# A Mamba layer's input projection as one product a half, with the causal convolution's taps on ScalarE and VectorE

## The chip, the cores and the metric

The kernel runs on one core of one Trainium2 chip. The metric is the time of one execution on the device in microseconds (us). A profile is one execution taken by the hardware profiler; PE is TensorE, DVE is VectorE, ACT is ScalarE, POOL is GpSimd, SP is SyncE, whose queue issues the DMAs.

## What is computed

Two "metaformer" layers over an image of 4 x 128 channels x 64 x 64. Layer 0 is a deformable neighbourhood attention, then a sigmoid recurrence over the 4,096 positions. Layer 1 is a stack of eight Mamba layers, then a mixture of experts. Only the Mamba layer is changed:

```
xz = x @ Wi                                  # (B, L, 128) @ (128, 512)
xi, z = split(xz, 2)                         # 256 inner channels each
xp = pad(xi, 3 zeros ahead along L)
xc = silu(sum(xp[:, k:k+L, :] * cw[:, k] for k in range(4)) + cb)
dt, Bs, Cs = from xc @ Wx                    # dt through softplus
h_t = exp(dt A) h_(t-1) + dt xc Bs           # 16 states per inner channel, a scan along L
y = (sum over states of h Cs + D xc) * silu(z)
out = y @ Wo, then RMS norm
```

Everything is float32.

## The kernel before

Four stages follow each other: the attention (`conv_layer`), the recurrence, `mamba`, the experts. The first two and the last are ordered by a scheduler, `mamba` is not: there each engine executes its instructions in the order of the program.

Channels lie on the 128 partitions, positions along the free dimension, in chunks of 512 (`TL`). The 256 inner channels are two halves (`h` = 0, 1). The unit of work is a body: one chunk, one layer, one image; there are 8 chunks x 8 layers x 4 images = 256 bodies. A body's work is spread over three turns of the main loop: `front(n, j)` prepares body n while body o = n - 1 is scanned, and `last(q, j)` finishes body q = o - 1. A turn has 16 slots (`j`); slot j handles two of the 16 states for one half:

- `decay` (L650, ScalarE) writes dA = exp(dt A) for slot j + 2, into four buffers;
- `inputs` (L664, TensorE) writes dt xc Bs into PSUM (dBx, two buffers of two banks) for slot j + 1, from `dtxT` and the block diagonal `diag`;
- `scan` (L679, VectorE) runs two scans into `hs`, from dA in SBUF and dBx in PSUM;
- `times_c` (L691 and L694, GpSimd) keeps the last state and multiplies `hs` by C, which lies in `Cb`;
- `add_up` (L715, TensorE) adds the products of slot j - 2 into `yT` in PSUM by transposing them. `skips` (L702) starts that sum in slot 2 with D xc, by a diagonal matrix.

Between these stand the steps of `front` and `last`. In `front`: `halo` (L532 and L533, GpSimd) puts the last three inputs of the chunk before in front of u, the layer's normalized input, and keeps this chunk's last three in `tail`; `proj` (L540, TensorE) makes projection and convolution of a half in one PSUM bank, as four products, one for each tap, each of a weight matrix already scaled by the tap with u shifted by one position. Two of them stand in each of slots 0, 1 (first half) and 3, 4 (second half). `silu` (L548 to L556) comes in slot 5, `xproj` (L563) in 6, `step_proj` (L587) in 8, `softplus` (L594) in 9, `turn_b` (L623) and `step_x` (L603, GpSimd) in 10, `diag` (L635, VectorE) in 11 and 12, `turn` (L613, L618) in 12 and 13. In `last`: `leave` (L729, ScalarE) copies `yT` in slot 1, `turn_back` transposes it (L735) and multiplies it by the gate on VectorE (L736) in slots 2 and 6, `out_proj` (L742 to L748) is in slot 7, `rms` (L752) in 10, `rms_u` (L757) in 11. All these PSUM results share two banks (`bank()`).

The tap-scaled weights are made once at the start: `mamba_weights` loads, for each layer, the projection and the taps spread over all partitions, multiplies them on GpSimd (L415), makes the diagonal matrices of D on VectorE (L419), and stores both to DRAM in `made_d` (L426), from which `load` fetches `made` and `given` for every layer, once in four bodies. These DMAs stand in SyncE's queue ahead of the first stage's own weights (L117 to L128). The first stage's depthwise convolution (L192) is a chain of 48 VectorE instructions a block, each of which reads two SBUF tensors.

Of the kernel before, what the change touches and what calls it, by code (L numbers as in the profile page):

```python
# [8 lines left out]
F32 = mybir.dt.float32  # L9
AF = mybir.ActivationFunctionType  # L10
ALU = mybir.AluOpType
# [6 lines left out]
P = 128  # L18
B = 4
# [18 lines left out]
DEPTH = 8  # L38
NH = 2
DI = NH * P  # L40
NS = 16
RK = 8
DC = 4
TL = 512
# [350 lines left out]

W_CONV, W_D, W_MADE = 0, DC * DI, DC * DI + NH * P
W_Z, W_X, W_DT, W_OUT, W_GIVEN = 0, DI, DI + NH * P, 2 * DI + NH * P, 2 * DI + 2 * NH * P


def mamba_weights(tc, ops, I, made_d):

    nc = tc.nc
    with tc.tile_pool(name="mw", bufs=2) as w:
        skip = w.tile([P, DEPTH, NH], F32, name="skip", bufs=1)
        nc.sync.dma_start(out=skip, in_=I["m_skip"])
        for l in range(DEPTH):
            wi = w.tile([P, DI], F32, tag="wi", name="wi")
            nc.sync.dma_start(out=wi, in_=I["m_in"][l])  # L410
            taps = w.tile([P, DC, DI], F32, tag="taps", name="taps")
            nc.sync.dma_start(out=taps, in_=I["m_taps"][l].partition_broadcast(P))
            made = w.tile([P, W_MADE], F32, tag="made", name="made")
            for t in range(DC):
                nc.gpsimd.tensor_tensor(  # L415
                    made[:, W_CONV + t * DI : W_CONV + (t + 1) * DI], wi, taps[:, t, :], ALU.mult
                )
            for h in range(NH):
                nc.vector.tensor_scalar(  # L419
                    made[:, W_D + h * P : W_D + (h + 1) * P],  # L420
                    ops.ident,
                    skip[:, l, h : h + 1],
                    None,
                    ALU.mult,
                )
            nc.sync.dma_start(out=made_d[l], in_=made)  # L426

# [9 lines left out]
def mamba(tc, ops, I, made_d, x2_d, x3_d):  # L437
# [7 lines left out]
    nc = tc.nc  # L445
# [3 lines left out]
    with ExitStack() as ctx:  # L449
        c = ctx.enter_context(tc.tile_pool(name="mc", bufs=1))  # L450
        wp = ctx.enter_context(tc.tile_pool(name="mwp", bufs=2))
        w1 = ctx.enter_context(tc.tile_pool(name="mw1", bufs=1))
        w = ctx.enter_context(tc.tile_pool(name="mwk", bufs=2))
# [3 lines left out]
        up = ctx.enter_context(tc.tile_pool(name="mu", bufs=6))  # L457
# [5 lines left out]
        cb = c.tile([P, DEPTH, NH], F32, name="cb")  # L463
# [9 lines left out]

        i64 = c.tile([P, 64], F32, name="i64")
        nc.vector.tensor_tensor(i64, ops.ident[:, 0:64], ops.ident[:, 64:P], ALU.add)

        tail = c.tile([P, DEPTH, B, DC - 1], F32, name="tail")
        nc.vector.memset(tail, 0.0)
        state = c.tile([P, DEPTH, B, NH, NS], F32, name="state")
        nc.vector.memset(state, 0.0)  # L480

        T0 = DC - 1
        us = {}
        weights = {}

        def bank():
            return psf.tile([P, TL], F32, tag="f", name="f")
# [28 lines left out]
            rstd(o.var, ops.eps6)  # L516

        def start_d(o):
            us[o.b] = up.tile([P, T0 + TL], F32, tag="u", name="u")
            nc.vector.tensor_tensor(us[o.b][:, T0:], o.xm, o.var, ALU.mult)  # L520

        def rstd(v, eps):

# [2 lines left out]
            nc.scalar.activation(v, r, AF.Exp, scale=-0.5)  # L526


        def halo(o):
            o.made, o.given = weights[o.l]  # L530
            o.u = us[o.b]
            nc.gpsimd.tensor_copy(o.u[:, 0:T0], tail[:, o.l, o.b, :])  # L532
            nc.gpsimd.tensor_copy(tail[:, o.l, o.b, :], o.u[:, TL : TL + T0])  # L533
            o.px = {}

        def proj(o, h, t):
            if t == 0:
                o.px[h] = bank()
            at = W_CONV + t * DI + h * P
            nc.tensor.matmul(  # L540
                o.px[h], o.made[:, at : at + P], o.u[:, t : t + TL], start=t == 0, stop=t == DC - 1
            )

        def silu(o):
            o.xc = w.tile([P, NH, TL], F32, tag="xc", name="xc")
            o.gate = w.tile([P, NH, TL], F32, tag="gate", name="gate", bufs=3)
            for h in range(NH):
                nc.scalar.activation(  # L548
                    o.xc[:, h, :], o.px[h], AF.Silu, bias=cb[:, o.l, h : h + 1]
                )  # L550
            for h in range(NH):
                pz = bank()
                at = W_Z + h * P
                nc.tensor.matmul(pz, o.given[:, at : at + P], o.u[:, T0:], start=True, stop=True)
                nc.scalar.activation(o.gate[:, h, :], pz, AF.Silu)
            nc.scalar.preload_act_table_set(EXP_LN)  # L556

# [24 lines left out]
        def step_proj(o):  # L582
            o.pt = {}
            for h in range(NH):
                o.pt[h] = bank()
                at = W_DT + h * P
                nc.tensor.matmul(  # L587
                    blocks(o.pt[h]), o.given[:, at : at + P], o.dbl, start=True, stop=True
                )
# [39 lines left out]
        def diag(o, n):  # L629

            if n == 0:
                o.diag = w.tile([P, NB, NS // 2, 64, 2], F32, tag="diag", name="diag")
            for k in range(2):
                at = n * P + RK + k
                nc.vector.tensor_tensor(  # L635
                    o.diag[:, n, :, :, k],
                    o.BT[:, at : at + NS : 2].unsqueeze(2).to_broadcast([P, NS // 2, 64]),
                    i64.unsqueeze(1).to_broadcast([P, NS // 2, 64]),
                    ALU.mult,
                )  # L640
# [55 lines left out]
        def skips(o):  # L696

            o.yT = psy.tile([P, NH, NB, P], F32, tag="yT", name="yT")
            for h in range(NH):
                at = W_D + h * P  # L700
                for n in range(NB):
                    nc.tensor.matmul(  # L702
                        o.yT[:, h, n, :],
                        o.xc[:, h, n * P : (n + 1) * P],
                        o.made[:, at : at + P],
                        start=n == 0,
                        stop=True,
                        skip_group_check=True,
                    )
# [43 lines left out]
            rstd(o.pm, ops.eps5)  # L753

        def rms_u(o):
            us[o.b] = up.tile([P, T0 + TL], F32, tag="u", name="u")
            nc.vector.tensor_tensor(us[o.b][:, T0:], o.pos, o.pm, ALU.mult)  # L757

        def end(o):
            here = (slice(None), o.b, slice(o.ck * TL, (o.ck + 1) * TL))  # L760
            x3 = w1.tile([P, TL], F32, tag="x3", name="x3")
            nc.sync.dma_start(out=x3, in_=x2_d[here])
            nc.gpsimd.tensor_tensor(x3, x3, us[o.b][:, T0:], ALU.add)
            nc.sync.dma_start(out=x3_d[here], in_=x3)


# [6 lines left out]
        def front(n, j):  # L773

            if j == 0:
                halo(n)
            if j in (0, 1):
                proj(n, 0, 2 * j)
                proj(n, 0, 2 * j + 1)
            elif j in (3, 4):  # L780
                proj(n, 1, 2 * (j - 3))
                proj(n, 1, 2 * (j - 3) + 1)
            elif j == 5:
                silu(n)
            elif j == 6:
                xproj(n)
            elif j == 8:
                step_proj(n)
            elif j == 9:
                softplus(n)  # L790
            elif j == 10:
                turn_b(n)
                step_x(n)
            elif j == 12:
                turn(n, 0)
            elif j == 13:
                turn(n, 1)
            if 11 <= j <= 12:
                diag(n, 2 * (j - 11))
                diag(n, 2 * (j - 11) + 1)  # L800
            if 8 <= j:
                give_c(n, j - 8)

        def last(q, j):

            if j == 1:
                leave(q)
            elif j == 2:
                turn_back(q, 0)
            elif j == 6:  # L810
                turn_back(q, 1)
            elif j == 7:
                out_proj(q)
            elif j == 10:
                rms(q)
            elif j == 11:
                rms_u(q)
            elif j == 12 and q.l == DEPTH - 1:
                end(q)
# [16 lines left out]
        for j in range(NSLOT):  # L836
            front(bodies[0], j)
# [3 lines left out]
        for i in range(len(bodies) + 1):  # L841
            o, n, q, s = get(i), get(i + 1), get(i - 1), get(i + 2)
# [210 lines left out]
def layouts(a):  # L1053
# [3 lines left out]
    def halves(v):  # L1057
        return np.moveaxis(v.reshape(DEPTH, NH, P, *v.shape[2:]), 2, 0)

    f = {k: np.asarray(v) for k, v in a.items()}  # L1060
    o = {}
# [16 lines left out]
    o["offw"] = offw  # L1078
    o["mask"] = attention_masks()
    w_in = f["L1_conv_W_in"]  # L1080
    o["m_in"] = w_in[:, :, :DI]
    o["m_taps"] = f["L1_conv_conv_w"].transpose(0, 2, 1)
    given = np.zeros((DEPTH, P, W_GIVEN), np.float32)
    given[:, :, W_Z : W_Z + DI] = w_in[:, :, DI:]
    for h in range(NH):
        ch = slice(h * P, (h + 1) * P)
# [9 lines left out]
    gate = np.zeros((P, 2, P), np.float32)  # L1096
# [24 lines left out]
```

## Time and profile before

| what | value |
|---|---|
| time, median of 3 runs | 24,200.53 us (24,181.13 to 24,201.42) |
| the profiled execution: its own time | 24,197.25 us |
| its span, from first to last instruction | 24,195.5 us |
| mean granted TensorE clock | 0.811 |
| busy over the span: PE, DVE, POOL, ACT | 83%, 56%, 50%, 45% |
| scans (L679) in the Mamba stage | 8,192, from 7,403.8 us on |

A line of the groups reads: line, engine, operation, output <- inputs by name, shapes, count | busy us, mean ns of one | idle time of the engine just before them, and what ended it. A line of the waits reads: who waited <- for whom: us in total, times, longest. A line of the timeline reads: start, duration, engine, line, operation. Two kinds of TensorE instruction are counted for each float32 product that is no transpose, so a product is two MATMUL instructions.

### The profile page before, as it was taken

How to read it: one execution, taken by the hardware profiler on the slowest of the kernel's cores; microseconds unless marked ns; L12 is line 12 of the kernel's file. 1: busy time of each engine (PE TensorE's matmuls, PEld its weight loads, DVE VectorE, ACT ScalarE, POOL GpSimd, SP SyncE). 2: the span in 40 equal slices, each digit the busy share in tenths (PEclk: the TensorE clock that was granted, in tenths of full speed). 3: DMA queues.
4: the chain of work that ended last, by engine and by line, in shares of the span. 5: the costliest groups of instructions: out<-in, count | busy, mean ns of one | idle time of the engine just before them, and what ended most of it. 6: DMA issues, size and time to landing. Idle time of an engine off the chain costs nothing. (4 is left out here: it accounts for less than half of the span.)

```text
span 24195.5 us, 332916 instructions
## 1 busy us (share of the span) xinstructions
PE 20047.8 (83%) x133890; PEld 14387.8 (59%) x133890; DVE 13649.9 (56%) x14587; ACT 10831.4 (45%) x19815; POOL 12077.8 (50%) x10464
## 2 busy tenths in 40 slices
PE   4775867666668899989898998989898898989887
PEld 2442435555556666666666666666666666666665
DVE  6446350000005777777777777777777777777771
ACT  2332332222224555555555555555555555555551
POOL 3122120000005666666666666666666666666661
PEclk6665655555558999999999999999999999999996
DMA  0000000000001222222222212222221222222223
GB/s 28 12 8 7 13 6 11 8 7 8 7 6 65 73 72 79 72 74 76 74 73 72 79 69 77 76 74 72 74 77 70 75 76 74 74 76 73 72 75 93
DMA packets 501522, 1334.68 MB, mean 55 GB/s; under 512 B 86416, under 2 KB 170000, under 8 KB 499856
## 3 DMA queue, kind: packets, MB, share of 16 engines
q1 hardware_dynamic: 499984, 1313.37, 15.7%
q8 instruction: 1063, 17.42, 0.3%
q14 instruction: 475, 3.89, 0.0%
HBM read 1257.59 MB, written 55.57 MB: 54 GB/s over the span
## 5 line engine op out<-in xcount | busy, mean ns | idle before, releaser
L679 DVE TENSOR_TENSOR_SCAN hs<-dA,state,dBx 128x512 f32<-128x512 f32 x8192 | 9856.6, 1262 | 2837.8 <-PE dBx L664 2354.5
L694 POOL TENSOR_TENSOR hs<-hs,Cb 128x1024 f32<-128x1024 f32 x4096 | 9655.6, 2357 | 329.3 <-POOL state L691 3.7
L664 PEld LDWEIGHTS dBx<-diag,dtxT 64*128 64x128 f32 x65536 | 4206.2, 196 | 3026.9 <-issue 1765.9
L650 ACT ACTIVATE dA<-dt,A 128x512 f32<-128x512 f32 x8192 | 5317.1, 715 | 1263.8 <-DVE hs L679 1243.8
L664 PE MATMUL dBx<-diag,dtxT 64*128 64x128 f32 x65536 | 5013.0, 294 | 826.2 <-DVE hs L679 825.2
L715 PE MATMUL yT<-ident,hs 128*128 128x128 f32 x32768 | 4653.8, 289 | 4.4 <-POOL hs L694 4.4
L715 PEld LDWEIGHTS yT<-ident,hs 128*128 128x128 f32 x32768 | 3704.9, 146 | 507.5 <-issue 81.7
L388 PE MATMUL p<-y,vt 128*128 128x4 f32 x8192 | 2411.8, 365 | 1069.0 <-ACT y L391 1069.0
L691 POOL COPY state<-hs 128x2 f32<-128x2 f32 x4096 | 768.6, 188 | 4751.5 <-DVE hs L679 4696.5
L540 PE MATMUL f<-u,made 128*128 128x512 f32 x4096 | 2366.7, 708 | 787.8 <-POOL u L532 787.8
L388 PEld LDWEIGHTS p<-y,vt 128*128 128x128 f32 x8192 | 2063.1, 313 | 1460.1 <-ACT y L391 1439.9
L391 ACT ACTIVATE y<-p 128x4 f32<-128x4 f32 x4096 | 711.2, 174 | 2826.2 <-PE p L388 2826.2
L393 POOL TENSOR_TENSOR x<-x,y 128x512 f32<-128x512 f32 x32 | 48.9, 1529 | 3497.8 <-ACT y L391 3497.8
L379 DVE TENSOR_SCALAR wx<-wx,sc,sh 128x512 f32<-128x512 f32 x32 | 17.5, 546 | 2975.6 <-DMA wx<-wx_d 2975.6
L540 PEld LDWEIGHTS f<-u,made 128*128 128x128 f32 x4096 | 798.5, 216 | 1464.6 <-POOL u L532 848.3
L729 ACT COPY yTs<-yT 128x512 f32<-128x512 f32 x512 | 274.9, 589 | 2743.1 <-PE yT L715 2743.1
L736 DVE TENSOR_TENSOR y<-f,gate 128x512 f32<-128x512 f32 x512 | 354.3, 692 | 1661.3 <-PE f L735 1661.3
L635 DVE TENSOR_TENSOR diag<-f,i 128x512 f32<-128x512 f32 x2048 | 1265.7, 684 | 12.7 <-PE f L623 12.7
L192 DVE SCALAR_TENSOR_TENSOR acc<-qp,dww,acc 128x512 f32<-128x512 f32 x1536 | 1177.7, 827 | 2.6
L618 ACT COPY dtxT<-f 128x512 f32<-128x512 f32 x512 | 300.1, 586 | 1218.0 <-PE f L613 1217.9
L296 PEld LDWEIGHTS pa<-vk,at 110*128 110x128 f32 (+1 forms) x3072 | 597.9, 289 | 201.6 <-ACT exps L280 125.7
L603 POOL TENSOR_TENSOR dtx<-dt,xc 128x512 f32<-128x512 f32 x512 | 648.0, 1288 | 18.6 <-ACT dt L594 18.6
(196 smaller groups left out, 16886.0 us busy)
## 6 DMA issues: line engine op xcount, KB each, us to landing
Cb<-c_d SPq DMA_DIRECT2D x2048, 512.0 KB, 4.1
x<-x_d SPq DMA_DIRECT2D x160, 256.0 KB, 2.9
made<-made_d SPq DMA_DIRECT2D x64, 640.0 KB, 5.6
given<-in_m_given_dram SPq DMA_DIRECT2D x64, 512.0 KB, 6.3
w<-in_w_dram SPq DMA_DIRECT2D x128, 256.0 KB, 2.7
x_d<-x SPq DMA_DIRECT2D x96, 256.0 KB, 2.0
xb<-in_x_dram SPq DMA_DIRECT2D x32, 256.0 KB, 2.6
xr<-in_x_dram SPq DMA_DIRECT2D x32, 256.0 KB, 2.7
```

What stands on the lines that cost most here:

```text
L192: nc.vector.scalar_tensor_tensor(rows(acc), qp[:, r + dy : r + dy + ROWS, dx : dx + W], dww[:, t : t + 1], rows(acc), ALU.mult, ALU.add,)
L388: nc.tensor.matmul(p[:, t, :], vt, before, start=False, stop=True, skip_group_check=True)
L391: nc.scalar.activation(y[:, t, :], p[:, t, :], AF.Sigmoid)
L540: nc.tensor.matmul(o.px[h], o.made[:, at : at + P], o.u[:, t : t + TL], start=t == 0, stop=t == DC - 1)
L603: nc.gpsimd.tensor_tensor(to, blocks(o.dt[:, h, :]), blocks(o.xc[:, h, :]), ALU.mult)
L635: nc.vector.tensor_tensor(o.diag[:, n, :, :, k], o.BT[:, at : at + NS : 2].unsqueeze(2).to_broadcast([P, NS // 2, 64]), i64.unsqueeze(1).t ...
L650: nc.scalar.activation(o.dA[j][:, k, :], o.dt[:, h, :], AF.Exp, scale=A[:, o.l, h, s : s + 1])
L664: nc.tensor.matmul(o.dBx[j][:, at : at + 64, :], o.dtxT[row, h, n, :], o.diag[row, n, sp], start=True, stop=True,)
L679: nc.vector.tensor_tensor_scan(hs[:, k, :], o.dA[j][:, k, :], o.dBx[j][:, :, k], state[:, o.l, o.b, h, s : s + 1], ALU.mult, ALU.add,)
L691: nc.gpsimd.tensor_copy(state[:, o.l, o.b, h, 2 * sp : 2 * sp + 2].unsqueeze(2), hs[:, :, TL - 1 : TL])
L694: nc.gpsimd.tensor_tensor(hs, hs, o.Cb[sp], ALU.mult)
L715: nc.tensor.matmul(o.yT[:, h, n, :], o.hs[j][:, k, n * P : (n + 1) * P], ops.ident, start=False, stop=True, is_transpose=True, skip_group_ ...
```

## The change

The projection is one product a half (`proj`, now with the plain weights, which move into `given`). ScalarE copies the bank into `xc`, scaled by the last tap. The other three taps are added into `xc` on VectorE (`tap`): one instruction for the positions that have their input in this chunk, read from PSUM, and one for the first one to three positions, read from `tail`, which now holds the projection's last three outputs and not u's. After the third tap, `tail` is renewed from PSUM. `silu` then works in place on `xc`. `halo`, the tap-scaled weights and the three extra columns of u are gone; `taps` is a small table in SBUF.

Some steps move: `turn_back` of the second half from slot 6 to slot 4, `diag` from two each in slots 11 and 12 to one each in slots 10 to 13. `gate` has two buffers and not three.

```diff
 def mamba_weights(tc, ops, I, made_d):
         for l in range(DEPTH):
-            wi = w.tile([P, DI], F32, tag="wi", name="wi")
-            nc.sync.dma_start(out=wi, in_=I["m_in"][l])
-            taps = w.tile([P, DC, DI], F32, tag="taps", name="taps")
-            nc.sync.dma_start(out=taps, in_=I["m_taps"][l].partition_broadcast(P))
             made = w.tile([P, W_MADE], F32, tag="made", name="made")
-            for t in range(DC):
-                nc.gpsimd.tensor_tensor(
-                    made[:, W_CONV + t * DI : W_CONV + (t + 1) * DI], wi, taps[:, t, :], ALU.mult
-                )
...
-        tail = c.tile([P, DEPTH, B, DC - 1], F32, name="tail")
+        taps = c.tile([P, DEPTH, NH, DC], F32, name="taps")
+        nc.sync.dma_start(out=taps, in_=I["m_taps"])
+        tail = c.tile([P, DEPTH, B, NH, DC - 1], F32, name="tail")
...
-        def halo(o):
-            o.made, o.given = weights[o.l]
-            o.u = us[o.b]
-            nc.gpsimd.tensor_copy(o.u[:, 0:T0], tail[:, o.l, o.b, :])
-            nc.gpsimd.tensor_copy(tail[:, o.l, o.b, :], o.u[:, TL : TL + T0])
-            o.px = {}
-
-        def proj(o, h, t):
-            if t == 0:
-                o.px[h] = bank()
-            at = W_CONV + t * DI + h * P
-            nc.tensor.matmul(
-                o.px[h], o.made[:, at : at + P], o.u[:, t : t + TL], start=t == 0, stop=t == DC - 1
+        def proj(o, h):
+            if h == 0:
+                o.made, o.given = weights[o.l]
+                o.u = us[o.b]
+                o.xc = w.tile([P, NH, TL], F32, tag="xc", name="xc")
+                o.v = {}
+            v = o.v[h] = bank()
+            at = W_I + h * P
+            nc.tensor.matmul(v, o.given[:, at : at + P], o.u, start=True, stop=True)
+            nc.scalar.activation(
+                o.xc[:, h, :], v, AF.Copy, scale=taps[:, o.l, h, DC - 1 : DC]
             )
+        def tap(o, h, k):
+            x, tl = o.xc[:, h, :], tail[:, o.l, o.b, h, :]
+            t = taps[:, o.l, h, DC - 1 - k : DC - k]
+            nc.vector.scalar_tensor_tensor(
+                x[:, k:], o.v[h][:, : TL - k], t, x[:, k:], ALU.mult, ALU.add
+            )
+            nc.vector.scalar_tensor_tensor(
+                x[:, :k], tl[:, DC - 1 - k :], t, x[:, :k], ALU.mult, ALU.add
+            )
+            if k == DC - 1:
+                nc.vector.tensor_copy(tl, o.v[h][:, TL - k :])
...
         def silu(o):
-            o.gate = w.tile([P, NH, TL], F32, tag="gate", name="gate", bufs=3)
+            o.gate = w.tile([P, NH, TL], F32, tag="gate", name="gate")
             for h in range(NH):
-                nc.scalar.activation(
-                    o.xc[:, h, :], o.px[h], AF.Silu, bias=cb[:, o.l, h : h + 1]
-                )
+                x = o.xc[:, h, :]
+                nc.scalar.activation(x, x, AF.Silu, bias=cb[:, o.l, h : h + 1])
...
         def front(n, j):
             if j == 0:
-                halo(n)
-            if j in (0, 1):
-                proj(n, 0, 2 * j)
-                proj(n, 0, 2 * j + 1)
-            elif j in (3, 4):
-                proj(n, 1, 2 * (j - 3))
-                proj(n, 1, 2 * (j - 3) + 1)
+                proj(n, 0)
+                tap(n, 0, 1)
+            elif j == 1:
+                tap(n, 0, 2)
+                tap(n, 0, 3)
+                proj(n, 1)
+            elif j == 2:
+                tap(n, 1, 1)
+                tap(n, 1, 2)
+            elif j == 3:
+                tap(n, 1, 3)
...
-            if 11 <= j <= 12:
-                diag(n, 2 * (j - 11))
-                diag(n, 2 * (j - 11) + 1)
+            if 10 <= j <= 13:
+                diag(n, j - 10)
...
         def last(q, j):
-            elif j == 6:
+            elif j == 4:
                 turn_back(q, 1)
```

More of the change, by code (lines that the diff above doesn't have):

```diff
@@ L394, in recurrence @@
             nc.sync.dma_start(out=x2_d[here], in_=x1)
-W_CONV, W_D, W_MADE = 0, DC * DI, DC * DI + NH * P
-W_Z, W_X, W_DT, W_OUT, W_GIVEN = 0, DI, DI + NH * P, 2 * DI + NH * P, 2 * DI + 2 * NH * P
+W_MADE = NH * P
+W_I, W_Z, W_X, W_DT = 0, DI, 2 * DI, 2 * DI + NH * P
+W_OUT, W_GIVEN = 3 * DI + NH * P, 3 * DI + 2 * NH * P
 def mamba_weights(tc, ops, I, made_d):
@@ L408, in mamba_weights @@
         for l in range(DEPTH):
-            wi = w.tile([P, DI], F32, tag="wi", name="wi")
-            nc.sync.dma_start(out=wi, in_=I["m_in"][l])
-            taps = w.tile([P, DC, DI], F32, tag="taps", name="taps")
-            nc.sync.dma_start(out=taps, in_=I["m_taps"][l].partition_broadcast(P))
             made = w.tile([P, W_MADE], F32, tag="made", name="made")
-            for t in range(DC):
-                nc.gpsimd.tensor_tensor(
-                    made[:, W_CONV + t * DI : W_CONV + (t + 1) * DI], wi, taps[:, t, :], ALU.mult
-                )
             for h in range(NH):
                 nc.vector.tensor_scalar(
[L420 to L424, printed above, removed]
+                    made[:, h * P : (h + 1) * P], ops.ident, skip[:, l, h : h + 1], None, ALU.mult
                 )
@@ L480, in mamba @@
         nc.vector.memset(state, 0.0)
-        T0 = DC - 1
         us = {}
@@ L518, in start_d @@
         def start_d(o):
-            us[o.b] = up.tile([P, T0 + TL], F32, tag="u", name="u")
-            nc.vector.tensor_tensor(us[o.b][:, T0:], o.xm, o.var, ALU.mult)
+            us[o.b] = up.tile([P, TL], F32, tag="u", name="u")
+            nc.vector.tensor_tensor(us[o.b], o.xm, o.var, ALU.mult)
         def rstd(v, eps):
@@ L526, in rstd @@
             nc.scalar.activation(v, r, AF.Exp, scale=-0.5)
-        def halo(o):
-            o.made, o.given = weights[o.l]
-            o.u = us[o.b]
-            nc.gpsimd.tensor_copy(o.u[:, 0:T0], tail[:, o.l, o.b, :])
-            nc.gpsimd.tensor_copy(tail[:, o.l, o.b, :], o.u[:, TL : TL + T0])
-            o.px = {}
-        def proj(o, h, t):
-            if t == 0:
-                o.px[h] = bank()
-            at = W_CONV + t * DI + h * P
-            nc.tensor.matmul(
-                o.px[h], o.made[:, at : at + P], o.u[:, t : t + TL], start=t == 0, stop=t == DC - 1
-            )
+        def proj(o, h):
[9 more added lines that the diff above has]
+                o.xc[:, h, :], v, AF.Copy, scale=taps[:, o.l, h, DC - 1 : DC]
+            )
+        def tap(o, h, k):
[9 more added lines that the diff above has]
+                nc.vector.tensor_copy(tl, o.v[h][:, TL - k :])
         def silu(o):
-            o.xc = w.tile([P, NH, TL], F32, tag="xc", name="xc")
-            o.gate = w.tile([P, NH, TL], F32, tag="gate", name="gate", bufs=3)
+            o.gate = w.tile([P, NH, TL], F32, tag="gate", name="gate")
             for h in range(NH):
-                nc.scalar.activation(
-                    o.xc[:, h, :], o.px[h], AF.Silu, bias=cb[:, o.l, h : h + 1]
-                )
+                x = o.xc[:, h, :]
+                nc.scalar.activation(x, x, AF.Silu, bias=cb[:, o.l, h : h + 1])
             for h in range(NH):
@@ L553, in silu @@
                 at = W_Z + h * P
-                nc.tensor.matmul(pz, o.given[:, at : at + P], o.u[:, T0:], start=True, stop=True)
+                nc.tensor.matmul(pz, o.given[:, at : at + P], o.u, start=True, stop=True)
                 nc.scalar.activation(o.gate[:, h, :], pz, AF.Silu)
@@ L699, in skips @@
             for h in range(NH):
-                at = W_D + h * P
+                at = h * P
                 for n in range(NB):
@@ L755, in rms_u @@
         def rms_u(o):
-            us[o.b] = up.tile([P, T0 + TL], F32, tag="u", name="u")
-            nc.vector.tensor_tensor(us[o.b][:, T0:], o.pos, o.pm, ALU.mult)
+            us[o.b] = up.tile([P, TL], F32, tag="u", name="u")
+            nc.vector.tensor_tensor(us[o.b], o.pos, o.pm, ALU.mult)
         def end(o):
@@ L762, in end @@
             nc.sync.dma_start(out=x3, in_=x2_d[here])
-            nc.gpsimd.tensor_tensor(x3, x3, us[o.b][:, T0:], ALU.add)
+            nc.gpsimd.tensor_tensor(x3, x3, us[o.b], ALU.add)
             nc.sync.dma_start(out=x3_d[here], in_=x3)
@@ L1080, in layouts @@
     w_in = f["L1_conv_W_in"]
-    o["m_in"] = w_in[:, :, :DI]
-    o["m_taps"] = f["L1_conv_conv_w"].transpose(0, 2, 1)
+    o["m_taps"] = halves(f["L1_conv_conv_w"])
     given = np.zeros((DEPTH, P, W_GIVEN), np.float32)
+    given[:, :, W_I : W_I + DI] = w_in[:, :, :DI]
     given[:, :, W_Z : W_Z + DI] = w_in[:, :, DI:]
```

## The prediction, made before the changed kernel ran

> **What bounds it now.** I read the stages first: busy time of each engine in a stretch of the Mamba stage (columns: length, then busy us and instruction count of PE, PEld, DVE, ACT, POOL, then the clock), then the groups of that stage with shapes apart, then who waited for whom between 10,000 and 20,000 us.
>
> ```profile
> 16000.00:19000.00 3000.00, 2698.40 (x21535) 1950.35 (x21531) 2135.95 (x2044) 1635.98 (x2425) 2049.43 (x1712) 0.93 0.21 73
> ```
> ```profile
> L679 DVE TENSOR_TENSOR_SCAN hs<-dA,state,dBx 128x512 f32<-128x512 f32 x5058 | 6086.3, 1262 | 1760.9 <-PE dBx L664 1461.7 <-ACT pos L748 215.0 <-POOL state L691 81.4
> L694 POOL TENSOR_TENSOR hs<-hs,Cb 128x1024 f32<-128x1024 f32 x2529 | 5961.6, 2357 | 203.3 <-POOL state L691 2.2
> L540 PE MATMUL f<-u,made 128*128 128x512 f32 x2533 | 1463.6, 708 | 488.2 <-POOL u L532 488.2
> L736 DVE TENSOR_TENSOR y<-f,gate 128x512 f32<-128x512 f32 x316 | 218.7, 692 | 1026.8 <-PE f L735 1026.8
> ```
> ```profile
> DVE hs L679 <- PE dBx L664: 1461.7, 540, 7.2
> DVE y L736 <- PE f L735: 1026.8, 316, 3.9
> PE dBx L664 <- DVE hs L679: 509.1, 474, 2.0
> PE f L540 <- POOL u L532: 488.2, 158, 3.6
> ```
>
> TensorE is busy 90%, VectorE 71%, GpSimd 68%. VectorE waits for TensorE, not the other way: 2,488 us over 158 bodies, 15.7 us each, against 6.3 us in which TensorE waits, half of them for the halo copy on GpSimd. The stage's first scan starts at 7,403.8 and its last at 23,564.3 us: 63.24 us a body once it runs steadily, in 256 bodies. TensorE sets the pace.
>
> Those waits cost twice. With narrow windows over one such gap (PEclk is third from the right) the clock falls to half just after it:
>
> ```profile
> 15100.00:15101.00 1.00, 0.66 (x6) 0.42 (x4) 1.00 (x2) 0.31 (x1) 1.00 (x1) 1.00 0.00 0
> 15101.00:15102.00 1.00, 0.00 (x0) 0.00 (x0) 1.00 (x2) 1.00 (x3) 0.89 (x1) 1.00 0.00 0
> 15102.00:15103.00 1.00, 0.47 (x8) 0.50 (x10) 1.00 (x3) 0.51 (x1) 0.47 (x2) 1.00 0.00 0
> 15104.00:15105.00 1.00, 1.00 (x6) 1.00 (x6) 1.00 (x3) 0.00 (x0) 1.00 (x1) 0.50 0.56 188
> ```
>
> The clock changes only on a grid of 3.41 us. Over this stage's 4,477 grid windows, one in which TensorE was busy under 0.49 was always followed by half clock, one over 0.50 never; out of half clock it came only after a window of 0.93 or more.
>
> **What goes.** Six of eight projection products a body: in the timeline, four instructions of L540 (two products) start 1.81 us before the next, so 12 of 16 instructions are 5.43 us at full clock. TensorE's sum of such steps falls from 52.6 to 47.1 us a body. The two halo copies (0.19 us each) leave GpSimd's queue, and with them TensorE's 3.1 us wait a body. The weight loads shrink (`made` 640 to 128 KB, `given` 512 to 640 KB); they are issued two bodies ahead of use at a DMA share of 0.21, so that gives nothing, and could at most give the 6 us that one takes to land, 64 times, if it were waited for, which no row shows. At the start, L415 holds up SyncE's queue, so that the convolution's weights (L119) are issued at 53.5 us; with only two diagonal products and one transfer a layer, four rounds of about 3.5 us leave them at about 17: 36 us less.
>
> **What comes.** On ScalarE two scaled copies a body, 0.68 us each by L748 (a Copy with a pointer scale), and Silu reads SBUF (L650's 715 ns against L548's 688): 35 becomes 36 us of 63, covered, except where VectorE waits for the copy. Gate with two buffers, not three: its last reader, the second L736, moves from slot 6 to slot 4, its writer stays in slot 5, so nothing. On VectorE: six large taps (PSUM in, pointer scalar), L338's form,
>
> ```profile
> L338 DVE SCALAR_TENSOR_TENSOR x<-po,vec,xr 128x512 f32<-128x512 f32 x32 | 24.0, 751 | 340.9 <-PE po L327 340.9
> ```
>
> 751 ns, 0.68 in a row; six taps of 1 to 3 elements, 0.21 (L368's 159 ns on 128x1 and 0.06 for the pointer, as 751 to 692); two tail copies, 0.13 in a row (L303: 175 alone). That is 4.1 + 1.3 + 0.3 = 5.6 us: VectorE has 45.0 + 5.6 = 50.6 us a body (45.0 is 2,136 of 3,000 us, by 63.24), and is now the longest: 50.6 is the floor of any walk, 24,197 - 256 x 12.6 = 20,970 us in all. A tap that waits holds up the next scans, which stand behind it in VectorE's queue; behind those wait GpSimd's L694, ScalarE's L650 (four dA buffers) and TensorE's L664 (two dBx buffers).
>
> The small taps read two tensors from SBUF (tail and xc). No VectorE instruction of the Mamba stage does so now (scan, diag, y and u each take one from PSUM, and keep 1 to 3% of their duration whatever GpSimd does). The first stage has some: L192, and in the timeline
>
> ```profile
> L192 DVE SCALAR_TENSOR_TENSOR acc<-qp,dww,acc x1536: 733/740/1755, 61.4 to 3302.1; 128x512 f32<-128x512 f32 x192
> ```
> ```profile
> 299.73 1.75 DVE L192 SCALAR_TENSOR_TENSOR acc<-qp,dww,acc 128x512 f32<-128x512 f32 x1
> ```
> ```profile
> 299.18 1.76 POOL L220 TENSOR_TENSOR t<-t,f 128x512 f32<-128x512 f32 x1
> ```
>
> 740 ns becomes 1,755 where a GpSimd instruction that reads SBUF was already running: VectorE ends 0.55 us after it. All 167 slow ones of 1,536 have such a one. So a small tap waits for the end of L694's 2.36 us if one runs. Bounds per body: 0 and 6 x 2.36 = 14.2 us; I take the full wait that L192's rows show, with the part of L694 that is left when the tap comes, slot by slot. No row has so short an instruction beside a running GpSimd one. The Trainium skill (SBUF — State Buffer, "Who interferes with whom") makes no exception for length: two SBUF inputs contend with a reading GpSimd instruction.
>
> **The walk.** I follow the queues through one body with the trace's durations. A slot is one pair of scans (2.35 us on VectorE). After it GpSimd needs 0.17 until the state copy starts and 0.27 more until L694, which ends 2.80 after VectorE went on. A large tap is done by 0.68, so its small one ends at 2.84. TensorE's slot is 1.09 (L664) + 0.95 (L715) + its extra products.
> - Slot 0: the product stands third on TensorE (0.2 + 1.09 + 0.95 + 0.90), then the copy: tap at 4.02 instead of 2.35; GpSimd, late from the body before (2.56 us a pair against 2.35 in slots 14 and 15), ends L694 at 5.4, then 0.2: 5.6 us.
> - Slot 1: 2.35 + 2.84 + second tap 0.89 + tail 0.13 = 6.2. Slot 2: 2.35 + 2.84 (y's 0.61 hidden in it) + 0.89 = 6.1. Slot 3: 2.35 + 2.84 + 0.13 = 5.3.
> - Slots 4 to 6: y 0.61 more in slot 4, with its transpose long done, as VectorE is now the later one (that ends the 6.5 us that L736 waits a body); else bare scans, then TensorE catches up: 3.0, 2.35, 2.4.
> - Slots 7 to 9: TensorE's 1.09 + 0.95 + 1.81 = 3.85 each, as now in slots 5, 8, 9 (3.83, 3.79, 3.83).
> - Slot 10: diag follows turn_b at once: TensorE, 0.73 behind, needs 1.09 + 0.95 + 0.86 + 0.53 = 3.43, +0.1, then 1.22: 5.5. Slot 11: 2.35 + 0.61 + 1.22 = 4.2; 12 and 13: 3.6 each; 14, 15: bare.
>
> ```
> slot     0    1    2    3    4    5    6    7    8    9    10   11   12   13   14   15    sum
> before   2.36 8.74 6.82 2.36 2.94 3.83 5.79 2.36 3.79 3.83 2.37 5.87 4.73 2.48 2.35 2.61  63.24
> after    5.6  6.2  6.1  5.3  3.0  2.35 2.4  3.85 3.85 3.85 5.5  4.2  3.6  3.6  2.35 2.35  64.1
> ```
>
> (Before: mean distance of scan pairs in the trace.) Slots 0 to 3 grow by 2.9, slots 4 to 9 give 3.2 back, slots 10 to 15 take 1.2. The waits at GpSimd are 0.8 + 1.95 + 1.35 + 1.95 = 6.0 of this. Half clock costs 2.3 now: the four L540 instructions of slot 0 take 3.41 and 3.78 us in two bodies of the timeline and 1.88 elsewhere, slot 1 is 8.74 where the same walk in the old order at full clock gives 6.73, and the other slots give 0.3. After, TensorE idles in slots 1 to 5; two windows a body fall under 0.49, mostly where VectorE is late anyway: 0.8 (bounds 0 and 2.3). Sum 64.9. The Trainium skill (TensorE: Matmul & The Clock Gate, "Part 1: The HAM clock gate") lets the clock fall only after a wholly idle window; my longest gap is 3.1 us, so by it this term were 0 and the total 205 us lower; the windows above contradict it.
>
> Total: 256 x (64.9 - 63.24) = +425, less 36: +389 on the profiled execution's own 24,197.25 us (span 24,195.5): **24,586**, and as the median, 24,200.53, lies 3 us above that, 24,590 us.
>
> **The rivals.** A, faster: an instruction of 1 to 3 elements is not held by GpSimd. For it: no row shows one held. Against: 167 of 167, and a held L192 waits before its first element. Slots 0 to 3 are then 4.9, 4.3, 4.7, 3.4 and the body 58.1: 24,197 - 1,316 - 36 = 22,850. The port's wait decides: 6.0 us of it make 6.8 of the body, so below 4.5 us a body the change is a gain. B, slower still: half clock reaches slots 6 to 9, where TensorE sets the pace, at today's price of 2.3 instead of 0.8: 66.4, 24,970. For it: leaving half clock takes a window of 0.93. C: the terms cancel (port wait 4.5 to 4.8, as taps that meet GpSimd later in L694 would have): 24,200.
>
> **The numbers.** Forecast 0.72 (24,400 to 24,800: body 64.1 to 65.7), A 0.13, B 0.10, C 0.05. The range runs from 24,330 to 24,970, with B in it and A out. A measurement tells 0.2% (48 us) from no change; faster 0.13, same 0.04, slower 0.83.
>
> **What would show it.** Right: L540 of the new kernel (small taps) with a mean near 1.2 us, a floor near 0.2 and a ceiling near 2.2; the new product group with 1,024 instructions; VectorE's busy time up by more than 256 x 5.6 us; "DVE y <- PE" nearly gone; the first-stage weights issued by 20 us. Wrong: small taps at 0.2 us throughout (then A), or PEclk under 0.85 in the stage (then B).

## The result, and the profile after

The changed kernel takes 24,563.1 us (median of 4 runs, 24,561.72 to 24,567.74), the kernel before 24,198.8 us beside it: ratio 1.0152, 95% interval 1.0135 to 1.017. That is 364 us slower; forecast were 389 us more, 24,590 us. The Mamba stage, from its first scan to its last, grew from 16,160.5 to 16,559.9 us, and it begins 29.8 us earlier (first scan at 7,374.0 us against 7,403.8).

The first view is the same stretch of the stage, busy time of each engine (PE, PEld, DVE, ACT, POOL, then the clock):

```profile
16000.00:19000.00 3000.00, 2389.29 (x20488) 1852.81 (x20488) 2587.82 (x2654) 1656.37 (x2463) 1997.93 (x1580) 0.94 0.20 70
```

TensorE fell from 90% to 80%, VectorE rose from 71% to 86%. The page's groups show the scans, which wait half as long as before (1,374 us in all against 2,838), and what has come to VectorE:

```profile
L679 DVE TENSOR_TENSOR_SCAN hs<-dA,state,dBx 128x512 f32<-128x512 f32 x8192 | 9941.2, 1262 | 1374.0 <-PE dBx L664 647.6
L540 DVE SCALAR_TENSOR_TENSOR xc<-tail,taps,xc 128x1 f32<-128x1 f32 (+2 forms) x1536 | 1813.0, 1180 | 0.0
L537 DVE SCALAR_TENSOR_TENSOR xc<-f,taps,xc 128x511 f32<-128x511 f32 (+2 forms) x1536 | 1125.1, 732 | 408.0 <-ACT xc L529 408.0
```

L540 is the small tap, of one to three elements a partition: it takes longer than L537, the large one of 509 to 511. This time is counted as busy; no view of waits shows it. It shows in the spread of L540's durations (minimum, median, maximum in ns), and in the timelines of VectorE and GpSimd over slot 1 of one body:

```profile
L540 DVE SCALAR_TENSOR_TENSOR xc<-tail,taps,xc x1536: 200/983/2269, 7354.6 to 23849.4; 128x1 f32<-128x1 f32 x64, 128x3 f32<-128x3 f32 x64, 128x2 f32<-128x2 f32 x64
```
```profile
15027.08 0.72 DVE L537 SCALAR_TENSOR_TENSOR xc<-f,taps,xc 128x510 f32<-128x510 f32 x1
15027.72 2.14 DVE L540 SCALAR_TENSOR_TENSOR xc<-tail,taps,xc 128x2 f32<-128x2 f32 x1
15029.79 0.73 DVE L537 SCALAR_TENSOR_TENSOR xc<-f,taps,xc 128x509 f32<-128x509 f32 x1
15030.45 0.20 DVE L540 SCALAR_TENSOR_TENSOR xc<-tail,taps,xc 128x3 f32<-128x3 f32 x1
```
```profile
15027.49 2.36 POOL L694 TENSOR_TENSOR hs<-hs,Cb 128x1024 f32<-128x1024 f32 x1
```

The first small tap begins at 15,027.72 while L694 runs, and ends at 15,029.86, 0.01 us after L694's end at 15,029.85. The second finds GpSimd idle and takes 0.20 us. Over the whole trace, 1,020 of the 1,536 small taps begin while such a GpSimd instruction runs; half of them end 18 ns or less after it, none over 96 ns. The other 516 take 200 to 209 ns. Together the small taps take 7.08 us a body, where 6 x 0.2 would be 1.2.

The waits between 10,000 and 20,000 us (154 bodies) have turned round:

```profile
PE dBx L664 <- DVE hs L679: 1960.5, 1358, 2.9
DVE hs L679 <- PE dBx L664: 397.8, 278, 3.1
DVE diag L635 <- PE f L623: 290.9, 155, 1.9
DVE xc L537 <- ACT xc L529: 244.9, 154, 1.7
```

TensorE now waits 12.7 us a body for VectorE, and VectorE 2.6 us for dBx. L736's wait for its transpose, 6.5 us a body before, is 2.8 us in the whole run. Two new waits appear, of 1.9 us in slot 10 (diag for turn_b) and 1.6 us in slot 0 (the first tap for ScalarE's copy).

The lengths of the slots, as the mean distance of scan pairs in the traces, beside the prediction's walk:

```
slot     0    1    2    3    4    5    6    7    8    9    10   11   12   13   14   15    sum
walk     5.6  6.2  6.1  5.3  3.0  2.35 2.4  3.85 3.85 3.85 5.5  4.2  3.6  3.6  2.35 2.35  64.1
after    5.46 6.05 5.87 5.30 2.95 2.36 3.67 3.85 3.81 3.83 5.53 4.14 3.54 3.65 2.36 2.41  64.8
```

### The profile page after: what moved, and what is told of

It reads as the page before. It is cut to its first block, busy times and chain, and to the rows that moved or that the text cites. A ratio compares the mean times of both kernels' runs of the same rounds, so it can differ in the third digit from the quotient of the medians.

```text
span 24561.9 us, 331388 instructions
## 1 busy us (share of the span) xinstructions
PE 18694.4 (76%) x130818; PEld 14092.8 (57%) x130818; DVE 16378.6 (67%) x18171; ACT 11145.8 (45%) x20327; POOL 12032.8 (49%) x9920
## 5 line engine op out<-in xcount | busy, mean ns | idle before, releaser
L694 POOL TENSOR_TENSOR hs<-hs,Cb 128x1024 f32<-128x1024 f32 x4096 | 9673.1, 2362 | 331.0 <-POOL state L691 6.0
L664 PE MATMUL dBx<-diag,dtxT 64*128 64x128 f32 x65536 | 5068.3, 296 | 3239.7 <-DVE hs L679 3239.2
L664 PEld LDWEIGHTS dBx<-diag,dtxT 64*128 64x128 f32 x65536 | 4285.9, 198 | 4983.5 <-issue 3670.3
L715 PE MATMUL yT<-ident,hs 128*128 128x128 f32 x32768 | 4872.3, 298 | 3.1 <-POOL hs L694 3.1
L715 PEld LDWEIGHTS yT<-ident,hs 128*128 128x128 f32 x32768 | 3948.2, 152 | 517.3 <-issue 104.9
L540 DVE SCALAR_TENSOR_TENSOR xc<-tail,taps,xc 128x1 f32<-128x1 f32 (+2 forms) x1536 | 1813.0, 1180 | 0.0
L537 DVE SCALAR_TENSOR_TENSOR xc<-f,taps,xc 128x511 f32<-128x511 f32 (+2 forms) x1536 | 1125.1, 732 | 408.0 <-ACT xc L529 408.0
L192 DVE SCALAR_TENSOR_TENSOR acc<-qp,dww,acc 128x512 f32<-128x512 f32 x1536 | 1177.6, 826 | 2.7
L555 ACT ACTIVATE gate<-f 128x512 f32<-128x512 f32 x512 | 305.7, 597 | 1519.6 <-PE f L554 1519.6
L529 ACT ACTIVATE xc<-f,taps 128x512 f32<-128x512 f32 x512 | 355.6, 695 | 1015.8 <-PE f L528 1015.8
```

Of the source, the lines that this page charges most:

```text
L192: nc.vector.scalar_tensor_tensor(rows(acc), qp[:, r + dy : r + dy + ROWS, dx : dx + W], dww[:, t : t + 1], rows(acc), ALU.mult, ALU.add,)
L537: nc.vector.scalar_tensor_tensor(x[:, k:], o.v[h][:, : TL - k], t, x[:, k:], ALU.mult, ALU.add)
L540: nc.vector.scalar_tensor_tensor(x[:, :k], tl[:, DC - 1 - k :], t, x[:, :k], ALU.mult, ALU.add)
L664: nc.tensor.matmul(o.dBx[j][:, at : at + 64, :], o.dtxT[row, h, n, :], o.diag[row, n, sp], start=True, stop=True,)
L694: nc.gpsimd.tensor_tensor(hs, hs, o.Cb[sp], ALU.mult)
L715: nc.tensor.matmul(o.yT[:, h, n, :], o.hs[j][:, k, n * P : (n + 1) * P], ops.ident, start=False, stop=True, is_transpose=True, skip_group_ ...
```

## The experiments

The ten kernels compare by their body, the mean distance of the first scans of two bodies. Each ratio is to runs of the kernel before that were made beside the version (for e7 their median was 24,175.1 us, else 24,197 to 24,199); e1 and e2 ran once:

| kernel | us | ratio to before (interval) | body, us |
|---|---|---|---|
| before | 24,198.8 | | 63.24 |
| after | 24,563.1 | 1.0152 (1.0135 to 1.0170) | 64.78 |
| e1, small taps read PSUM | 22,646.7 | one run | 57.32 |
| e2, small taps first | 24,024.9 | one run | 62.70 |
| e3, dBx twice in slots 1 to 4 | 24,319.3 | 1.0052 (1.0037 to 1.0067) | 63.85 |
| e4, diag back | 24,156.8 | 0.9984 (0.9974 to 0.9993) | 63.23 |
| e5, small taps on GpSimd | 22,516.9 | 0.9304 (0.9288 to 0.9320) | 56.80 |
| e6, that and diag back | 22,226.6 | 0.9184 (0.9171 to 0.9198) | 55.64 |
| e7, before, halo on ScalarE | 22,855.4 | 0.9455 (0.9439 to 0.9471) | 57.96 |
| e8, e6 and the first tap later | 21,985.4 | 0.9087 (0.9071 to 0.9102) | 54.71 |

### e1: the small taps read one SBUF tensor instead of two

```diff
             nc.vector.scalar_tensor_tensor(
-                x[:, :k], tl[:, DC - 1 - k :], t, x[:, :k], ALU.mult, ALU.add
+                x[:, :k], o.v[h][:, :k], t, x[:, :k], ALU.mult, ALU.add
             )
```

> Edit: the six small taps of a body read PSUM (the product's first columns) in place of tail, so that each takes one tensor from SBUF instead of two; same count, sizes, order and engine. The first three positions of a chunk then get other values. Port theory (a small tap waits because it reads two SBUF tensors while GpSimd reads SBUF): small taps near 0.2 us each, slots 0 to 3 at 4.9, 4.2, 4.7, 3.3 us, the body 57.9 to 58.2 us against 64.8, 22,800 to 22,870 us. Rival theory (a chain of tiny dependent instructions costs some 1.2 us each whatever it reads): nothing changes, 24,560 us.

This version isolates a cost and is no kernel to use: the first one to three positions of a chunk get wrong inputs.

The groups of e1:

```profile
L540 DVE SCALAR_TENSOR_TENSOR xc<-f,taps,xc 128x3 f32<-128x3 f32 x512 | 107.1, 209 | 0.0
L540 DVE SCALAR_TENSOR_TENSOR xc<-f,taps,xc 128x2 f32<-128x2 f32 x512 | 106.7, 208 | 0.0
L540 DVE SCALAR_TENSOR_TENSOR xc<-f,taps,xc 128x1 f32<-128x1 f32 x512 | 106.5, 208 | 0.0
```

With nothing changed but where the first operand lies, 1,180 ns become 208, and the kernel is 1,916 us faster than the changed one. Slots 0 to 3 are 4.82, 3.98, 4.51 and 3.19 us. Tiny instructions are not dear; the rival theory falls. (The body is 0.6 us under the expected 57.9, as unheld small taps cost some 0.13 us in a row, not 0.21.) The saving of 7.5 us a body exceeds the 5.9 us of waits, because the half clock goes with them: from 7,500 to 22,000 us it holds 11% of the time in the changed kernel, 2% in e1.

### e2: the same instructions in another order

```diff
             elif j == 1:
+                edge(n, 0, 2)
+                edge(n, 0, 3)
                 tap(n, 0, 2)
                 tap(n, 0, 3)
                 proj(n, 1)
```

and likewise in slots 0, 2 and 3. `edge` is the small tap, taken out of `tap`, which keeps the large one and the tail copy.

> Edit: the same instructions, but in each slot the small taps go ahead of the large ones, so that in slots 1 and 3 they start right after the scans, before L694 of that slot has begun (0.44 us after VectorE went on). In slot 2 y (0.6 us) still comes first, and in slot 0 the tap waits for ScalarE's copy. Port theory: slots 1 and 3 fall from 6.05 and 5.3 us to about 4.3 and 3.4; slot 2 stays at 5.9 to 6.7; slot 0 grows from 5.5 to about 6.2, the large tap now behind the waiting small one; the body near 63.1 us, 24,140 us. Theory that the added instructions themselves are the cost: no slot changes, 24,560 us.

Slots 0 to 3 are 6.12, 4.36, 6.90 and 3.20 us: the two that were to fall fell, by 1.7 and 2.1, slot 0 grew, slot 2, where a small tap still comes behind y, grew by 1.0, and slot 4 by 1.5. In these last two y waits for its transpose again, 2.4 us a body (10,000 to 20,000 us, 159 bodies):

```profile
DVE y L741 <- PE f L740: 374.6, 311, 2.4
```

The groups tell of the small taps by size. A body has two taps of each size; those of one element stand in slots 0 and 2, those of two in 1 and 2 (in slot 2 right behind the small tap that is held), those of three in 1 and 3:

```profile
L547 DVE SCALAR_TENSOR_TENSOR xc<-tail,taps,xc 128x1 f32<-128x1 f32 x512 | 678.5, 1325 | 406.2 <-ACT xc L529 406.1
L547 DVE SCALAR_TENSOR_TENSOR xc<-tail,taps,xc 128x3 f32<-128x3 f32 x512 | 106.9, 209 | 9.0
L547 DVE SCALAR_TENSOR_TENSOR xc<-tail,taps,xc 128x2 f32<-128x2 f32 x512 | 105.1, 205 | 9.1
```

Where a small tap gets in ahead of L694, it takes its 0.2 us. The theory that the added instructions themselves are the cost falls: here are the same ones, for 538 us less.

### e3: more work for TensorE

```diff
-            for n in range(NB):
+            for _ in range(2 if 2 <= j <= 5 else 1):
+                for n in range(NB):
...
```

> Edit: in slots 1 to 4 TensorE computes the next slot's dBx twice (32 products of L664 more a body, 4.4 us of work at full clock; the second writes the same values over the first). Clock theory (TensorE idles so long in slots 1 to 4 that windows of 3.41 us fall under 0.49, and the half clock that follows makes slot 6 3.7 us where the full clock would need 2.4): more work there lifts the windows, slot 6 falls to 2.4 us, body 64.0, 24,350 us, 0.9% faster with more work. Rival (the clock plays no part, TensorE's idle time just takes the work): 24,560 us, no change. Second rival (TensorE's work lies on the path): up to 4.4 us a body more, 25,690 us.

It is faster than the changed kernel by 244 us, with 4.4 us more products a body:

```profile
16000.00:19000.00 3000.00, 2488.64 (x23820) 1956.71 (x23816) 2622.30 (x2689) 1683.99 (x2504) 2029.84 (x1603) 0.98 0.21 72
```

The clock rose from 0.94 to 0.98 and slot 6 fell from 3.67 to 2.73 us, not quite to the expected 2.4; no other slot moved by over 0.04. Both rivals fall: TensorE's work in slots 1 to 4 is not on the path, and its idling there has a price, 0.94 us a body.

### e4: diag back in slots 11 and 12

```diff
-            if 10 <= j <= 13:
-                diag(n, j - 10)
+            if 11 <= j <= 12:
+                diag(n, 2 * (j - 11))
+                diag(n, 2 * (j - 11) + 1)
```

> Edit: only the move of diag is undone: two each in slots 11 and 12 again instead of one each in slots 10 to 13. Walk: slot 10 falls from 5.5 to 2.35 us, as VectorE no longer waits for turn_b, slots 11 and 12 are 5.7 and 4.8 as before the change, the sum of slots 10 to 13 falls by 0.8 to 1.3 us: body 63.6 to 64.0, 24,260 to 24,360 us. Rival (the move pays, since it spreads VectorE's work): slower than 24,563 us.

It gives more than expected, 406 us: slots 10 to 13 take 15.44 us and not 16.86, slot 6 falls to 3.23, and slot 15 takes 0.27 us back. Without this move the change would have been a draw: a body of 63.23 us against 63.24 before, 42 us faster in all, by the shorter start. Yet slots 0 to 3 are 2.5 us longer than before and slots 4 to 9 shorter by the same; the equality is a coincidence of sums. (That 24,157 lies outside the expected 24,260 to 24,360 us is a miss: 0.8 to 1.3 us were expected of slots 10 to 13, which gave 1.42, and slot 6 was left at 3.67.)

### e5 and e6: the small taps on GpSimd, and diag back

```diff
         def tap(o, h, k):
...
-            nc.vector.scalar_tensor_tensor(
-                x[:, :k], tl[:, DC - 1 - k :], t, x[:, :k], ALU.mult, ALU.add
-            )
...
+        def edges(o):
+            for k in range(1, DC):
+                m = w.tile([P, NH, k], F32, tag=f"m{k}", name="m")
+                nc.gpsimd.tensor_tensor(
+                    m,
+                    tail[:, o.ck % 2, o.l, o.b, :, DC - 1 - k :],
+                    taps[:, o.l, :, DC - 1 - k : DC - k].to_broadcast([P, NH, k]),
+                    ALU.mult,
+                )
+                nc.gpsimd.tensor_tensor(o.xc[:, :, :k], o.xc[:, :, :k], m, ALU.add)
...
                     scan(o, j)
+                    if n is not None and j == 4:
+                        edges(n)
                     times_c(o, j)
```

> Edit: the small taps move to GpSimd, in slot 4 ahead of its state copy, as six products and sums for both halves at once (about 0.2 us each); tail has two copies, by odd and even chunk, so that nobody waits to renew it. VectorE keeps the large taps and the tail copies, and reads two SBUF tensors nowhere. Port theory: slots 0 to 3 at 4.7, 3.8, 4.3, 3.1 us, body 56.7 us, 22,500 us: faster than the kernel before by 7%. Rival (GpSimd's queue gets too late by the 1.2 us and L715 or Silu waits for it): body above 58 us, over 22,830 us.

> Edit: the same, and diag back in slots 11 and 12. Walk: slots 10 to 13 give another 1.0 us: body 55.7 us, 22,240 us. Rival: TensorE's slots 7 to 10 (3.85 us each) take up the gain, since slot 10 is then TensorE's: as with the small taps on GpSimd alone, 22,500 us.

22,516.9 and 22,226.6 us: both as walked, to within 20 us. Slots 0 to 3 are 4.63, 3.85, 4.41 and 3.07 us. The six GpSimd instructions take 0.2 us each. They begin when GpSimd would else wait for the scans, and the slots behind them are no longer than in e1 (2.94, 2.36 and 2.43 us for slots 4 to 6 in both). Two of their groups in e5:

```profile
L549 POOL TENSOR_TENSOR m<-tail,taps 128x6 f32<-128x6 f32 x256 | 53.1, 207 | 0.0
L555 POOL TENSOR_TENSOR xc<-xc,m 128x6 f32<-128x6 f32 x256 | 51.5, 201 | 20.4 <-DVE xc L537 0.4
```

In e6 diag's old place gives 290 us more, so that rival falls too.

### e7: the kernel before, without its wait for the halo

```diff
         def halo(o):
-            nc.gpsimd.tensor_copy(o.u[:, 0:T0], tail[:, o.l, o.b, :])
-            nc.gpsimd.tensor_copy(tail[:, o.l, o.b, :], o.u[:, TL : TL + T0])
+            nc.scalar.copy(o.u[:, 0:T0], tail[:, o.l, o.b, :])
+            nc.scalar.copy(tail[:, o.l, o.b, :], o.u[:, TL : TL + T0])
```

> Edit: the kernel before, with nothing of the change but that the two halo copies go from GpSimd's queue to ScalarE's: all eight products stay on TensorE, no tap comes to VectorE. It asks what the change could have won by relieving TensorE, and which part of it. Theory 1 (the products are the smaller part: TensorE's wait for the halo, behind GpSimd's late L694, and the half clock after it, make slot 1 8.7 us): slot 1 falls to about 3.4 us, the body from 63.2 to 58.0 us, 22,890 us, so that the 5.4 us of products bring only the rest, some 2.3 us a body, down to the 55.6 us of the version with its small taps on GpSimd and diag back. Theory 2 (TensorE's amount of work is the bound, 52.6 us a body of products at full clock in a body of 63.2): the wait only moves to the next product, the body stays within 1 us of 63.2, above 23,940 us.

22,855.4 us, with all eight products on TensorE. Slot 1 falls from 8.74 to 3.40 us, the only slot that moves by over 0.2. The projection's group says how:

```profile
L540 PE MATMUL f<-u,made 128*128 128x512 f32 x4096 | 1930.0, 593 | 2.8 <-issue 2.8
```

Its 4,096 instructions take 593 ns in the mean and not 708, and the 788 us that TensorE sat idle before them are 2.8: 3.1 us of wait and 1.7 us of longer products a body, 4.8 of the 5.3 us that the body lost. Theory 2 falls: the amount of TensorE's work was not what made slot 1 long.

### e8: the first tap a slot later

```diff
             if j == 0:
                 proj(n, 0)
-                tap(n, 0, 1)
             elif j == 1:
+                tap(n, 0, 1)
                 tap(n, 0, 2)
```

on top of e6.

> Edit: the version with its small taps on GpSimd and diag back, and the first large tap moves from slot 0 to slot 1, so that VectorE does not wait in slot 0 for the product and ScalarE's copy (1.7 us a body in the changed kernel's trace). Walk: slot 0 falls from 4.8 to 2.35 us, slot 1 grows by the tap's 0.7, slot 2 by up to 0.7, where y now waits for the bank that the later taps free; body 54.6 us, 21,960 us. Rival (the wait in slot 0 only moves to slots 1 and 2, since TensorE and ScalarE are as late there): body 55.6 us, 22,220 us.

21,985.4 us, the fastest version. Slot 0 falls from 4.80 to 2.35 us, slots 1 and 2 grow from 3.85 and 4.41 to 4.62 and 4.91, slot 4 by 0.25: the body falls by 0.93 us, so over half of the 1.7 us that VectorE waited in slot 0 does not move along, and the rival falls. In this version TensorE is busy 91% and VectorE 90%:

```profile
16000.00:19000.00 3000.00, 2729.67 (x24238) 2113.10 (x24240) 2701.05 (x2811) 1962.66 (x2927) 2414.04 (x2202) 0.96 0.24 84
```

## Why the prediction was right

**The port.** The prediction took L192's waits in the first stage for the small taps' price, 6.0 us a body. Measured are 7.08 less 1.2, that is 5.9, in slots 0 to 3 0.64, 1.93, 1.35 and 1.94 us where 0.8, 1.95, 1.35 and 1.95 were walked, and e1 and e2 show the cause from two sides, the operand's place and the moment of issue. What no row of before could show, that an instruction of one element is held like one of 512, is so. The Trainium skill (SBUF — State Buffer, "Who interferes with whom") agrees with the 1,020 held taps and the 18 ns: the second SBUF input goes through a read port shared with GpSimd, and whoever comes second is held for the other's whole instruction.

The prediction read the rows of L192 too broadly, though: the recorded start of GpSimd's instruction does not tell who is held. Of the 1,536 in the trace before, another 158 began while L97, a GpSimd instruction with two SBUF inputs, was on record as running, and kept their 733 to 752 ns. There L97 was the slow one, with up to 8.46 us where the shortest of this group take 1.26:

```profile
342.97 8.46 POOL L97 TENSOR_TENSOR on<-xm,rstd 128x512 f32<-128x512 f32 x1 [4.87 <-ACT rstd L77]
```

The small taps met no such case: all 1,020 that began beside a running L694 ended after it, and L694 kept its 2.34 to 2.39 us.

**The walk.** The slots came out at 5.46, 6.05, 5.87 and 5.30 us against 5.6, 6.2, 6.1 and 5.3; of the difference of 0.5 some 0.3 are large taps, an unheld small tap and tail copies, which follow each other by 0.65, 0.13 and 0.09 us where 0.68, 0.21 and 0.13 were taken; the rest is not traced. Slots 7 to 13 are right to 0.1 us each.

**Half clock.** Taken were 0.8 us a body, in no certain slot; it sits in slot 6 (3.67 us against 2.43 in e1, which hardly has half clock), 1.25 us, of which e3 gets 0.94 back. So this term was too small by 0.45 us a body. Rival B, that it would reach the slots in which TensorE sets the pace, happened in one slot of four. The rule read from before was too sharp: in the trace after, windows of up to 0.50 busy were followed by half clock, while some down to 0.42 were not, and half clock was left after windows of 0.81. The Trainium skill (TensorE: Matmul & The Clock Gate, "Part 1: The HAM clock gate") has the half clock come after at least one idle window of some 3.4 us, which the prediction took for a window without any work. In this trace TensorE's longest idle stretch between 8,000 and 21,500 us is 2.9 us, where 3.1 was foreseen, and yet the clock fell 417 times, after windows of at least 0.15 busy; the measurement decides against the rule so read.

**The start.** 30 us, forecast 36: L119 is issued at 19.70 us and not 53.52, where 17 was forecast. The first scans of e1 to e6 and e8, with the same start, lie between 7,361.5 and 7,371.8 us, so this term is known to some 10 us only.

**Where the gain went.** The prediction read "TensorE sets the pace" off the waits, and named the halo's wait as half of TensorE's own. e7 shows how much hung on it: 3.1 us of wait, with the half clock behind it, were 5.3 us a body (63.24 to 57.96). In e6 the change is worth 63.24 - 55.64 = 7.6 us a body, of which e7 has 5.3 without removing a single product. Taken in this order, six products, 5.4 us of TensorE's time, and what else moved bring the other 2.3, net of VectorE's added work; no run removes the products alone. From e6 back to the changed kernel the ladder is: diag moved, 55.64 to 56.80 (e5), 1.2 us; small taps on VectorE but not held, to 57.32 (e1), 0.5; held by GpSimd, to 64.78, 7.5.

The sum has its large parts right, the port's wait and the slots that TensorE sets. That it came within 27 us of the measured time is luck: slots 0 to 3 were walked 0.5 us too long and the half clock taken 0.45 us too short, some 120 us each over 256 bodies, and the two cancel. Without the port's wait the change would have been a gain: e1, with one operand in PSUM, is 6.4% faster than the kernel before, and e5, which computes the right thing, 7.0%.

## What to carry to other kernels

Before an elementwise step goes to VectorE in a kernel with GpSimd at work, count its SBUF tensor inputs: with two of them even a one-element instruction waited here for the end of the GpSimd instruction that was reading SBUF, and the profile books that as busy time, not as a wait. Ask of a wait first who is late, and whether the waiting step can change queues: here two copies of three elements, moved from one queue to another, gave 5.5%, while the rewrite of the arithmetic around them, as it was first written, cost 1.5%. And when a step is moved a slot, look at what it reads: diag moved one slot forward landed on the heels of its producer, for 1.2 to 1.6 us a body.

## What the runs showed of the hardware that was not expected

- More work can be faster: 32 products more a body in TensorE's idle time (e3) took 244 us off; the clock of the stage rose with them from 0.94 to 0.98.
- The waits do not shorten with the instruction: 128x1, 128x2 and 128x3 have means of 1,196, 1,170 and 1,174 ns in the changed kernel, against 208 to 209 ns when one operand lies in PSUM.
- The clock's threshold is not one number in the busy time that this trace shows: it fell after windows of up to 0.50 and held after some of 0.42. What it goes by is open.
